# Graph attention in two layers on one core: the probabilities of head 2 turned by VectorE in six tiles of eight, and the order around head 4

## The chip, the cores and the metric

One core of a Trainium2 chip runs the whole program. The metric is device time in microseconds of one execution, from launch to end; the kernel before and the changed kernel are each run several times. Engines named below: TensorE (PE in the profile; its weight loads PEld), VectorE (DVE), ScalarE (ACT), GpSimd (POOL), and SyncE (SP), whose queue starts most of the DMAs here. Each engine takes its instructions in the order in which the program lists them, and waits where one of them has to wait.

## The reference

Sixteen graphs of 1024 nodes with 256 features pass through two layers, each with a residual. Layer 0 is masked attention with 8 heads of 32 features; layer 1 is a softmax over the products of the normed nodes, chosen by the kind of edge.

```python
h = jnp.maximum(_layernorm(x), 0.0)              # (16, 1024, 256)
Q, K, V = proj(Wq, bq), proj(Wk, bk), proj(Wv, bv)   # 8 heads of 32
scores = jnp.where(adj == 0, -inf, einsum('bhnd,bhmd->bhnm', Q, K) * 32 ** -0.5)
x = x + einsum('bno,po->bnp', heads_joined(softmax(scores) @ V), Wo) + bo

h = jnp.maximum(_layernorm(x), 0.0)
e_k = leaky_relu(einsum('bid,bjd->bij', h * a_k, h), 0.2)     # k = 0..3
scores = e_{adj - 1} where adj is 1..4, else -9e15
x = x + softmax(scores) @ h
```

In these inputs `adj` is 0 or 1, so layer 1 needs only `e_0`; a general version stands behind a test at the end of the program and isn't run.

## The kernel before, in words

Rows are worked in tiles of 128: eight tiles `t` to a batch, sixteen batches `b`, one after another in steps `s = 8 b + t`. The order of all instructions is written out by hand (`tc.manual_schedule()`, from L787 on): the loop over `s` (L839) has an inner loop over the heads `h` from 0 to 7 (L863), and each pass of it lists what is to be done at that place. Five things are under way at once: `now`, the attention tile whose scores are made; `was`, the tile before, whose products with the values are finished at heads 0 to 6; `gone`, the tile before that, whose normed result is turned; `edge` and `edge_was`, two tiles of layer 1, nine steps behind; and `piece_was` and `piece`, tiles whose queries, keys and values are projected nine steps ahead.

A head of an attention tile passes through these steps. `scores(h)` (L457) is two matmuls into one of two PSUM places, `sides[0]` or `sides[1]`; from step 9 on heads 4 and 6 use `sides[1]`, the others `sides[0]`, and the scores of layer 1 (`edge.score`, heads 0 and 2) use `sides[1]` too. `softmax_max(h)` (L469) on VectorE adds the mask, finds the maximum and writes a buffer `p`, of which there are four in turn. `softmax_exp(h - 1)` (L479) on ScalarE follows one pass later. Then the 128x1024 probabilities are turned so that keys lie on the partitions, in one of two ways:

- `turn` (L492, L585): eight TensorE transposes through PSUM, and two copies to `pT`, by ScalarE or, for a head of `MIXED`, by VectorE.
- `turn_blocks` and `place_blocks` (L379, L384): one VectorE instruction turns all blocks of 32x32 within 32 partitions, into one of three buffers `blocks`, and four DMAs of 128 KB from SP's queue bring the four groups of partitions to their places in `pT`. The keys of such a `pT` stand in another order ("blocks' order").

`combine(g)` (L522) multiplies four turned heads by their values `v` into one PSUM bank; `combine(0)` is at head 7 of the tile itself, `combine(1)` at head 4 of the next, in `block()` (L850). `combined` multiplies by the reciprocals of the sums, which GpSimd spreads (`reciprocals`), TensorE turns (`turn_reciprocals`) and ScalarE copies (`turned_reciprocals`, L518).

Values in blocks' order come from `hTm`, a copy of the turned input `hT` with its columns in that order; `values` (L335) makes 128 columns from the one and 128 from the other, and `place_of` says where a head's 32 columns lie. `MIXED` names the heads whose values are in blocks' order, (0, 1, 4, 5). `by_blocks(t)` names those that are turned by blocks: all of `MIXED`, except in tile 7 (0, 1, 4) and in tile 0 (0, 4, 5). Where a head is in the one set and not in the other, its exponential writes into a further `p` in changed order (L482).

A tile of layer 1 has its own steps: `score`, `keep` (ScalarE saves blocks of the symmetric scores in `mirror` for later tiles, L641), `softmax_max` into `sel`, `bend`, `leak`, `softmax_exp`, then in the next step `turn_blocks` and `place_blocks` at head 0, `gather(0)` (L694) in `block()`, `gather(1)` and `store` at head 7. `gather` needs the placed `pT` of all four DMAs.

Two loads on SP's queue matter. `load_queries` (L425) brings the next tile's queries `qt` (512 KB) at head 3. `load_key` (L357) brings the keys of one head (512 KB) of the next batch: `KEY_STEPS` (L78) says for each key at which half pass, counted from tile 7's head 0 as 0 and with 16 as the next batch's tile 0, it is issued.

PSUM places named `sums_place` and `brief` share one tile, `early` and `late` another (L94); the program waits by tile, so a write to one of a pair also waits for a reader of the other.

Of the kernel before, what the change touches and what calls it, by code (L numbers as in the profile page):

```python
# [17 lines left out]
P = 128  # L18
HEADS = 8
HD = 32  # L20
# [3 lines left out]
SLOPE = 0.2  # L24
NEG_INF = -9000000000000000.0
MASKED = -1e30
MIXED = (0, 1, 4, 5)
BY_BLOCKS = {7: (0, 1, 4), 0: (0, 4, 5)}


def by_blocks(t):
    return BY_BLOCKS.get(t, MIXED)


def place_of(h):

    return (h // 2 % 2) * P + (h // 4) * 2 * HD + (h % 2) * HD


FLOOR = 1e28  # L40


# [5 lines left out]
def gnn_kernel(  # L48
# [19 lines left out]
    B, N, D = x.shape  # L68
    NT = N // P
    NC = D // P  # L70
# [4 lines left out]
    LEAD = NT + 1  # L75


    KEY_STEPS = (6, 9, 10, 13, 16, 20, 22, 24)  # L78
    KEPT = LAG + 1

    const = ctx.enter_context(tc.tile_pool(name="const", bufs=1))
# [27 lines left out]
    bv_t = const.tile([P, D], F32, name="bv_t")  # L109
    bo_t = const.tile([P, D], F32, name="bo_t")  # L110

    def load_biases():
        with nc.allow_non_contiguous_dma(reason="a few hundred elements, once"):
            nc.sync.dma_start(out=bq_t, in_=bq.rearrange("(c p) -> p c", p=P))
            nc.sync.dma_start(out=bk_t, in_=bk.rearrange("(c p) -> p c", p=P))
            for k, a in enumerate((a_0, a_1, a_2, a_3)):
                nc.sync.dma_start(out=a_t[:, :, k], in_=a.rearrange("(c p) o -> p (c o)", p=P))
        for i in range(2):
            nc.sync.dma_start(
                out=bv_t[:, i * P : (i + 1) * P].rearrange("p (r d) -> p r d", r=2),  # L120
                in_=bv.rearrange("(r i d) -> i r d", i=2, r=2)[i].partition_broadcast(P),
            )
        nc.sync.dma_start(out=bo_t, in_=bo.partition_broadcast(P))

# [7 lines left out]
    def transposed_weight(name, copy=nc.vector.tensor_copy):  # L132

        rows = weight_rows[name]
        wt = const.tile([P, NC, D], F32, name=name)
        tr = ps_tr.tile([P, 4, P], F32, tag="tr", name=f"{name}_tr")
        for fc in range(NC):
            for oc in range(NC):
                nc.tensor.transpose(tr[:, fc * NC + oc, :], rows[:, oc, fc * P : (fc + 1) * P], ident)
        if name == "wvT":  # L140
            for fc in range(NC):
                nc.vector.tensor_copy(
                    wt[:, fc].rearrange("p (i r d) -> p r i d", i=2, r=2),
                    tr[:, fc * NC : (fc + 1) * NC].rearrange("p r (i d) -> p r i d", i=2),
                )
        else:
            copy(wt.rearrange("p c f -> p (c f)"), tr.rearrange("p c f -> p (c f)"))
        return wt
# [37 lines left out]
    qds, kds, vs, keysets, weights = {}, {}, {}, {}, {}  # L186

    class Piece:
# [146 lines left out]
        def values(self):  # L335
            b = self.b
            if b not in vs:
                vs[b] = graph.tile([P, NT, D], F32, tag="v", name=f"v_{b}")
            for t in range(self.n):
                ps = late if self.n == 1 else ps_tr.tile([P, D], F32, tag="tr", name="vproj")  # L340
                self.vproj = ps
                for i, hT in enumerate((self.hTm, self.hT)):
                    for fc in range(NC):
                        nc.tensor.matmul(
                            ps[:, i * P : (i + 1) * P],
                            lhsT=hT[:, fc, t * P : (t + 1) * P],
                            rhs=weights["wvT"][:, fc, i * P : (i + 1) * P],
                            start=(fc == 0),
                            stop=(fc == NC - 1),
                        )  # L350
                if self.n > 1:
                    self.biased(t)
# [423 lines left out]
    def attend_of(s):  # L776
        return Attend(*divmod(s, NT)) if 0 <= s < B * NT else None
# [9 lines left out]
    with tc.manual_schedule():  # L787
        first = [Piece(0, 0, 4), Piece(0, 4, 4)]
        piece_was, piece_next = Piece(1, 0), piece_of(0)
        now, nxt = attend_of(0), attend_of(1)  # L790
# [39 lines left out]
        piece, edge, edge_was = piece_next, None, None  # L830
# [8 lines left out]
        for s in range(B * NT + 1):  # L839
            b, t = divmod(s, NT)  # L840
# [5 lines left out]
                    load_key(b, KEY_STEPS.index(2 * (HEADS + h) + end))  # L846

            late_turn = None

            def block():  # L850
                if edge_was and not t:
                    edge_was.gather(0)
                if was:
                    was.combine(1)
                if not t and piece_was:
                    piece_was.biased()
                if was:
                    was.combined()
                if edge_was and t:
                    edge_was.gather(0)  # L860

            nxt2, edge_nxt, piece_nxt = attend_of(s + 2), edges_of(s + 1), piece_of(s + 1)
            for h in range(HEADS):  # L863
# [12 lines left out]
                    first[1].values()  # L876
                if h == 3 and edge:
                    edge.softmax_max()
                if h == 6:
                    if was:  # L880
                        was.residual()
                    norms(was, piece_nxt)
# [13 lines left out]
                if ending:  # L896
                    ending.softmax_exp(eh)

                if h == 3 and edge:
                    edge.keep(1)  # L900
                if h == 3 and was:
                    was.turned_reciprocals()
                if h == 3 and piece_was:
                    piece_was.raised(1)
                if h == 3 and edge:
                    edge.bend()


                if h == 3 and t and piece_was:
                    piece_was.biased()  # L910
                if h == 5 and was:
                    was.output()
# [8 lines left out]
                if h == 0 and t == 0 and was:  # L921
                    for half in range(2):
                        was.turn(HEADS - 3, half, nc.scalar.copy)
                    if edge:
                        edge.score(0)
                if turning and th in by_blocks(turning.t):
                    turning.turn_blocks(th)
                    turning.place_blocks(th)
                elif turning and (h, t) != (HEADS - 1, NT - 1):
                    turning.turn(th, 0)  # L930
                    turning.turn(th, 1)
# [29 lines left out]
                        was.turn_reciprocals()  # L961
                        was.add_bias()
                if h == 3:
                    if nxt:
                        nxt.load_queries()
                    if edge:
                        edge.leak()
                    if piece_was:
                        piece_was.halve(1)
                    if edge_was:  # L970
                        edge_was.load_nodes()
                    if nxt:
                        nxt.flag()
                        nxt.mask()
                if h == 4:
                    block()
                if h == 5:
                    if piece_was:
                        piece_was.write_queries()
                    if edge_nxt:  # L980
                        edge_nxt.prepare()
                    if nxt2:
                        nxt2.load()
# [18 lines left out]
            gone, was, now, nxt = was, now, nxt, nxt2  # L1002
            edge_was, edge = edge, edge_nxt
            piece_was, piece = piece, piece_nxt
# [7 lines left out]
        for i in range(1, len(tiles) + 2):  # L1012
            edge = tiles[i] if i < len(tiles) else None
# [75 lines left out]
```

## Time and profile before

| what | us |
|---|---|
| median of three runs | 3014.63 (3009.04 to 3017.09) |
| the profiled execution | 3012.56 |
| its span, first to last instruction | 3010.7 |
| granted TensorE clock | 0.998 of full speed |

| instruction (line) | engine | count | mean ns |
|---|---|---|---|
| maximum of a head, `softmax_max` (L473) | VectorE | 1024 | 1209 |
| exponential of a head (L490) | ScalarE | 1024 | 1196 |
| block transpose of a head, `blocks<-p` (L381) | VectorE | 488 | 1240 |
| block transpose of `sel` (L381) | VectorE | 120 | 1241 |
| transposes on TensorE, `trp<-ident,p` (L590) | TensorE | 4352 | 274 |
| their copies (L591) | ScalarE | 1024 | 592 |
| their copies (L591) | VectorE | 64 | 685 |
| `pT<-blocks`, 128 KB, issue to landing | SP's queue | 2432 | 3600 (median) |
| `qt<-qd`, 512 KB, issue to landing | SP's queue | 128 | 4700 (median) |
| `k<-kd`, 512 KB, issue to landing | SP's queue | 128 | 6800 (median) |

How to read it: a line of a timeline gives the start in us from the span's start, the length, the engine, the line of the program, the operation, what is written and what is read with shapes, the count of instructions merged, and in brackets how long the engine had been idle before and what ended that. Matmuls overlap, so the distance from one start to the next tells more than a length (274 ns is one transpose's, but eight take about 0.8 us). The views of waits count idle time by what ended it. A page's share of busy time is a mean over stages with different limits; the timelines show which wait ends last in each.

### The profile page before, as it was taken

Reading aid. Unit: us, or ns where it says so; the run is one execution under the profiler, and the core shown is the slowest. Engines: PE = TensorE matmul, PEld = TensorE weight load, DVE = VectorE, ACT = ScalarE, POOL = GpSimd, SP = SyncE. Lnnn points to the kernel's source line nnn. Section 1 sums busy time; section 2 is a strip of 40 time slices with the busy share of each in tenths; the row PEclk is TensorE's granted clock in tenths of the full one; section 3 lists DMA queues with packets and bytes.
Section 4 is the critical chain, followed back from the end, with each engine's and each line's share of the span. In section 5 each row is a group of like instructions: output and inputs, shape, how many; then the busy total and the mean of one; then the engine's idle time right before and its main releaser. Section 6 shows DMA issues by size and latency. Waiting matters only on the chain. (4 is left out here: it accounts for less than half of the span.)

```text
span 3010.7 us, 95592 instructions
## 1 busy us (share of the span) xinstructions
PE 2888.7 (96%) x36466; PEld 2218.8 (74%) x36466; DVE 2517.8 (84%) x4421; ACT 2602.5 (86%) x5159; POOL 2167.4 (72%) x2999
## 2 busy tenths in 40 slices
PE   7889999999999999999999999999999999999998
PEld 5767777777777777777777777777777777777664
DVE  5878888788888888888888788888888888888885
ACT  5989989899898889889899898998989888898882
POOL 4667877777787787778778777777877777786542
PEclk9999999999999999999999999999999999999999
DMA  7787878878778887887877788787787878878763
GB/s 257 235 258 215 244 240 241 256 226 266 230 228 255 238 268 216 243 253 227 274 227 232 243 240 262 223 261 241 226 259 240 266 216 241 258 224 263 198 175 102
DMA packets 616255, 712.41 MB, mean 237 GB/s; under 512 B 65328, under 2 KB 546992, under 8 KB 615792
## 3 DMA queue, kind: packets, MB, share of 16 engines
q1 hardware_dynamic: 546720, 494.08, 55.5%
q0 software_dynamic: 66960, 210.04, 21.6%
q8 instruction: 293, 4.80, 0.7%
q10 hardware_dynamic: 2112, 2.10, 0.2%
q14 instruction: 170, 1.39, 0.1%
HBM read 252.98 MB, written 134.22 MB: 129 GB/s over the span
## 5 line engine op out<-in xcount | busy, mean ns | idle before, releaser
L473 DVE CUSTOM_DVE_ANT_0 p<-s,neg 128x1024 f32<-128x1024 f32 x1024 | 1237.9, 1209 | 320.2 <-PE s L461 291.9
L490 ACT ACTIVATE p<-p,nmx 128x1024 f32<-128x1024 f32 x1024 | 1218.3, 1196 | 53.3 <-DVE nmx L473 51.1
L461 PE MATMUL s<-k,qt 128*128 128x512 f32 x2048 | 743.7, 445 | 56.0 <-DMA k<-kd 28.4
L591 ACT COPY pT<-trp 128x512 f32<-128x512 f32 x1024 | 549.9, 592 | 99.9 <-PE trp L590 99.6
L381 DVE STREAM_TRANSPOSE blocks<-p 128x1024 f32<-128x1024 f32 x488 | 605.0, 1240 | 12.3 <-ACT p L680 10.6
L590 PE MATMUL trp<-ident,p 128*128 128x128 f32 x4352 | 571.5, 274 | 20.4 <-ACT p L490 13.0
L590 PEld LDWEIGHTS trp<-ident,p 128*128 128x128 f32 x4352 | 502.6, 141 | 105.0 <-ACT p L490 26.5
L526 PE MATMUL acc<-pT,v 128*32 128x128 f32 x16384 | 509.7, 274 | 11.3 <-ACT full L309 8.8
L526 PEld LDWEIGHTS acc<-pT,v 128*32 128x32 f32 x16384 | 454.7, 110 | 83.4 <-issue 36.9
L698 PE MATMUL acc<-h,pT 128*32 128x256 f32 x8192 | 508.4, 381 | 2.1 <-DMA pT<-blocks 2.0
L441 POOL TENSOR_SCALAR neg<-adj 128x1024 bf16<-128x1024 int32 x128 | 467.7, 3654 | 11.9 <-ACT neg L453 1.8
L461 PEld LDWEIGHTS s<-k,qt 128*128 128x128 f32 x2048 | 312.0, 190 | 182.7 <-issue 91.1
L676 POOL TENSOR_TENSOR sel<-sel,less 128x1024 f32<-128x1024 f32 x120 | 287.6, 2396 | 194.6 <-ACT less L665 194.6
L698 PEld LDWEIGHTS acc<-h,pT 128*32 128x32 f32 x8192 | 263.3, 110 | 191.9 <-issue 50.3
L633 PE MATMUL s<-h1T,ha 128*128 128x512 f32 (+2 forms) x744 | 272.8, 490 | 2.6 <-ACT h1T L569 0.8
L490 ACT ACTIVATION_READ_ACCUMULATOR p<-p,nmx 128x1 f32 x1024 | 211.8, 207 | 0.0
L330 POOL DMA_DIRECT2D kd<-halves x240 | 171.7, 764 | 35.4 <-POOL halves L314 35.4
L314 POOL TENSOR_TENSOR halves<-full,halves 128x256 fp32r<-128x256 f32 x240 | 176.3, 735 | 20.0
L647 ACT COPY mirror<-s 128x128 f32<-128x128 f32 (+3 forms) x208 | 75.9, 392 | 125.5 <-DVE top L656 104.4
L324 POOL DMA_DIRECT2D qd<-halves x240 | 177.3, 785 | 7.1
L674 POOL TENSOR_SCALAR less<-top 128x1 f32<-128x1 f32 x120 | 31.8, 265 | 204.3 <-DVE top L656 204.1
L633 PEld LDWEIGHTS s<-h1T,ha 128*128 128x128 f32 x744 | 126.7, 190 | 70.5 <-issue 45.2
(117 smaller groups left out, 4314.5 us busy)
## 6 DMA issues: line engine op xcount, KB each, us to landing
pT<-blocks SPq DMA_DIRECT2D x2432, 128.0 KB, 3.6
qt<-qd SPq DMA_DIRECT2D x128, 512.0 KB, 4.7
k<-kd SPq DMA_DIRECT2D x128, 512.0 KB, 6.8
adj<-in_adj POOLq DMA_DIRECT2D x127, 512.0 KB, 6.2
qd<-halves POOLq DMA_DIRECT2D x240, 256.0 KB, 3.8
kd<-halves POOLq DMA_DIRECT2D x240, 128.0 KB, 4.2
xb<-in_x POOLq DMA_DIRECT2D x128, 128.0 KB, 4.9
x1d<-x SPq DMA_DIRECT2D x128, 128.0 KB, 5.1
```

Source lines behind the costliest of these rows:

```text
L324: nc.gpsimd.dma_start(out=qds[self.b][self.first, oc].rearrange("p u w n -> p u (w n)"), in_=halves.unsqueeze(1).to_broadcast([P, 2, 2 * P]),)
L381: nc.vector.transpose(blocks.rearrange("p b j q -> p j b q"), p)
L441: nc.gpsimd.tensor_scalar(self.neg, self.adj, 0.0, MASKED, ALU.is_equal, ALU.mult)
L461: nc.tensor.matmul(self.ps[:, cols], lhsT=self.qt[:, h, :], rhs=keysets[self.b][h][:, cols], start=True, stop=True,)
L473: nc.vector.tensor_tensor_reduce(out=p, in0=sides[h in self.second], in1=self.neg, scale=-SCALE, scalar=FLOOR, op0=ALU.add, op1=ALU.min, a ...
L490: nc.scalar.activation(to, of, AF.Exp, bias=nmx, scale=-1.0, accum_out=self.sums[:, h : h + 1])
L526: nc.tensor.matmul(sums_place[r * HD : (r + 1) * HD, g * P : (g + 1) * P], lhsT=vs[self.b][:, j, place_of(h) : place_of(h) + HD], rhs=self ...
L590: nc.tensor.transpose(tr[:, j, :], p[:, jj * P : (jj + 1) * P], ident)
L591: copy(pT[:, half * 4 : half * 4 + 4, :], tr)
L633: nc.tensor.matmul(self.side[:, cols], lhsT=self.ha[:, c, :], rhs=h1T[:, c, cols], start=(c == 0), stop=(c == NC - 1),)
L676: nc.gpsimd.tensor_tensor(self.sel, self.sel, self.less, ALU.subtract)
L698: nc.tensor.matmul(self.sums[a * HD : (a + 1) * HD, :], lhsT=self.pT[:, j, a], rhs=h1s[self.b][:, j, :], start=(j == 0), stop=(j == NT - 1),)
```

## The change

- Head 2 joins `MIXED`: its values are made from `hTm` (160 columns from it, 96 from `hT`), its columns move, and the weights and bias are laid out by runs of heads (`RUNS`) with four copies and four DMAs where there were two.
- In tiles 1 to 6 (`five`) head 2 is turned by blocks. In tiles 0 and 7 it isn't, so that its exponential writes into a further `p` in changed order; in tile 7 the copies of its turn are VectorE's (in tile 0 they were already).
- In tiles 1 to 6 `block()` comes ahead of head 2's turn and head 4's scores and not behind them; `biased` (VectorE) comes ahead of head 3's maximum; `keep(1)` (ScalarE) comes behind the reciprocals' copy and `raised(1)`.
- `load_queries` moves from head 3 to head 5, except in tile 7.
- The fourth key's load moves from step 13 to step 12, the start of tile 7's head 6 and not its end.

```diff
@@ -24,7 +24,8 @@
 SLOPE = 0.2
 NEG_INF = -9000000000000000.0
 MASKED = -1e30
-MIXED = (0, 1, 4, 5)
+MIXED = (0, 1, 2, 4, 5)
+PLACES = MIXED + (3, 6, 7)
 BY_BLOCKS = {7: (0, 1, 4), 0: (0, 4, 5)}
 
 
@@ -33,10 +34,10 @@
 
 
 def place_of(h):
-
-    return (h // 2 % 2) * P + (h // 4) * 2 * HD + (h % 2) * HD
-
-
+    return PLACES.index(h) * HD
+
+
+RUNS = ((0, 0, 3), (3, 4, 2), (5, 3, 1), (6, 6, 2))
 FLOOR = 1e28
 
 
@@ -75,7 +76,7 @@
     LEAD = NT + 1
 
 
-    KEY_STEPS = (6, 9, 10, 13, 16, 20, 22, 24)
+    KEY_STEPS = (6, 9, 10, 12, 16, 20, 22, 24)
     KEPT = LAG + 1
 
     const = ctx.enter_context(tc.tile_pool(name="const", bufs=1))
@@ -115,10 +116,10 @@
             nc.sync.dma_start(out=bk_t, in_=bk.rearrange("(c p) -> p c", p=P))
             for k, a in enumerate((a_0, a_1, a_2, a_3)):
                 nc.sync.dma_start(out=a_t[:, :, k], in_=a.rearrange("(c p) o -> p (c o)", p=P))
-        for i in range(2):
+        for to, first, n in RUNS:
             nc.sync.dma_start(
-                out=bv_t[:, i * P : (i + 1) * P].rearrange("p (r d) -> p r d", r=2),
-                in_=bv.rearrange("(r i d) -> i r d", i=2, r=2)[i].partition_broadcast(P),
+                out=bv_t[:, to * HD : (to + n) * HD],
+                in_=bv[first * HD : (first + n) * HD].partition_broadcast(P),
             )
         nc.sync.dma_start(out=bo_t, in_=bo.partition_broadcast(P))
 
@@ -138,10 +139,10 @@
             for oc in range(NC):
                 nc.tensor.transpose(tr[:, fc * NC + oc, :], rows[:, oc, fc * P : (fc + 1) * P], ident)
         if name == "wvT":
-            for fc in range(NC):
+            rows = tr.rearrange("p (f o) n -> p f (o n)", f=NC)
+            for to, first, n in RUNS:
                 nc.vector.tensor_copy(
-                    wt[:, fc].rearrange("p (i r d) -> p r i d", i=2, r=2),
-                    tr[:, fc * NC : (fc + 1) * NC].rearrange("p r (i d) -> p r i d", i=2),
+                    wt[:, :, to * HD : (to + n) * HD], rows[:, :, first * HD : (first + n) * HD]
                 )
         else:
             copy(wt.rearrange("p c f -> p (c f)"), tr.rearrange("p c f -> p (c f)"))
@@ -339,12 +340,13 @@
             for t in range(self.n):
                 ps = late if self.n == 1 else ps_tr.tile([P, D], F32, tag="tr", name="vproj")
                 self.vproj = ps
-                for i, hT in enumerate((self.hTm, self.hT)):
+                edge = len(MIXED) * HD
+                for cols, hT in ((slice(0, edge), self.hTm), (slice(edge, D), self.hT)):
                     for fc in range(NC):
                         nc.tensor.matmul(
-                            ps[:, i * P : (i + 1) * P],
+                            ps[:, cols],
                             lhsT=hT[:, fc, t * P : (t + 1) * P],
-                            rhs=weights["wvT"][:, fc, i * P : (i + 1) * P],
+                            rhs=weights["wvT"][:, fc, cols],
                             start=(fc == 0),
                             stop=(fc == NC - 1),
                         )
@@ -846,6 +848,7 @@
                     load_key(b, KEY_STEPS.index(2 * (HEADS + h) + end))
 
             late_turn = None
+            five = now and 2 in by_blocks(t)
 
             def block():
                 if edge_was and not t:
@@ -876,6 +879,8 @@
                     first[1].values()
                 if h == 3 and edge:
                     edge.softmax_max()
+                if h == 3 and five and piece_was:
+                    piece_was.biased()
                 if h == 6:
                     if was:
                         was.residual()
@@ -896,17 +901,19 @@
                 if ending:
                     ending.softmax_exp(eh)
 
-                if h == 3 and edge:
+                if h == 3 and edge and not five:
                     edge.keep(1)
                 if h == 3 and was:
                     was.turned_reciprocals()
                 if h == 3 and piece_was:
                     piece_was.raised(1)
+                if h == 3 and edge and five:
+                    edge.keep(1)
                 if h == 3 and edge:
                     edge.bend()
 
 
-                if h == 3 and t and piece_was:
+                if h == 3 and t and not five and piece_was:
                     piece_was.biased()
                 if h == 5 and was:
                     was.output()
@@ -923,6 +930,8 @@
                         was.turn(HEADS - 3, half, nc.scalar.copy)
                     if edge:
                         edge.score(0)
+                if five and h == 4:
+                    block()
                 if turning and th in by_blocks(turning.t):
                     turning.turn_blocks(th)
                     turning.place_blocks(th)
@@ -961,7 +970,7 @@
                         was.turn_reciprocals()
                         was.add_bias()
                 if h == 3:
-                    if nxt:
+                    if nxt and t and not five:
                         nxt.load_queries()
                     if edge:
                         edge.leak()
@@ -972,9 +981,11 @@
                     if nxt:
                         nxt.flag()
                         nxt.mask()
-                if h == 4:
+                if h == 4 and not five:
                     block()
                 if h == 5:
+                    if nxt and (five or not t):
+                        nxt.load_queries()
                     if piece_was:
                         piece_was.write_queries()
                     if edge_nxt:
```

## The prediction

> **What bounds the kernel now.** I read the summary first, for how full each engine is:
>
> ```profile
> PE 2888.7 (96%) x36466; PEld 2218.8 (74%) x36466; DVE 2517.8 (84%) x4421; ACT 2602.5 (86%) x5159; POOL 2167.4 (72%) x2999
> ```
>
> TensorE (PE) is busy almost throughout, which says where to look and not what a saved microsecond is worth. The chain of waits holds only the last 20 us, so I read the timelines of one tile instead: batch 8, tile 4, from head 0's scores at 1568.62 to the next tile's at 1590.74. TensorE around head 4, where the change works:
>
> ```profile
> 1576.60 0.72 PE L461 MATMUL s<-k,qt 128*128 128x512 f32 x2
> 1577.16 1.04 PE L590 MATMUL trp<-ident,p 128*128 128x128 f32 x8
> 1578.24 0.73 PE L461 MATMUL s<-k,qt 128*128 128x512 f32 x2
> 1578.91 1.95 PE L526 MATMUL acc<-pT,v 128*32 128x128 f32 x64
> 1580.68 1.91 PE L698 MATMUL acc<-h,pT 128*32 128x256 f32 x32
> 1582.52 0.73 PE L461 MATMUL s<-k,qt 128*128 128x512 f32 x2
> ```
>
> That is: head 3's scores, head 2's eight transposes, head 4's scores, `combine(1)`, `gather(0)`, head 5's scores. The transposes cost 0.79 us from start to start where nothing waits (tile 1: 1510.46 to 1511.25); here 1.08, because head 4's scores wait for ScalarE's mirror copy, which itself waited on VectorE:
>
> ```profile
> 1577.61 0.59 ACT L647 COPY mirror<-s 128x512 f32<-128x512 f32 x1 [0.98 <-DVE top L656]
> ```
>
> VectorE (DVE) has its largest gap there too, waiting for head 5's scores:
>
> ```profile
> 1583.29 1.23 DVE L473 CUSTOM_DVE_ANT_0 p<-s,neg 128x1024 f32<-128x1024 f32 x1 [1.23 <-PE s L461]
> ```
>
> Next the view that decides: what `gather(0)` stands on. It multiplies the graph tile's probabilities (`sel`), which VectorE turns at the tile's start and SP's DMAs put in place. SP's queue from head 4's pieces on, and the gather of tile 5:
>
> ```profile
> 1588.58 3.98 SPq L386 DMA_DIRECT2D pT<-blocks  x4
> 1592.61 0.61 SPq L552 DMA_DIRECT2D x1d<-x  x1
> 1593.33 2.58 SPq L386 DMA_DIRECT2D pT<-blocks  x4
> 1596.49 0.60 SPq L708 DMA_DIRECT2D out<-h  x1
> ```
>
> ```profile
> 1602.73 2.78 PE L698 MATMUL acc<-h,pT 128*32 128x256 f32 x32
> ```
>
> The four issues for `sel` follow at 1597.21, 4.4 us after VectorE began that transpose (1592.76). They need 2.6 us and land some 2.7 later: 1602.5. The gather took 2.78 us where it takes 1.91: it started and then stood for a piece. So TensorE is full, but in this order the gather comes just as its pieces arrive. Over batches 2 to 14 the trace gives the last `sel` piece 11.3 us after head 0's scores in tiles 2 to 6 and the gather's start at 12.6, 12.3, 12.1, 11.9, 11.8. The tiles last 22.96, 22.65, 22.32, 22.16, 22.05, 21.92 (1 to 6), 22.21 (7) and 26.58 us (0).
>
> **The change, part by part.** The sum goes against the profiled run's own 3012.56 us (span 3010.7); the median of the three runs is 2.07 above it.
>
> *Tiles 1 to 6, engine work.* TensorE loses eight transposes and, as head 4's scores now come after the gather, the mirror wait: about 0.8 us in tile 1 and 1.0 to 1.2 in the others. ScalarE loses two copies (592 ns each). VectorE gains a block transpose, 1.16 us from start to start (1589.55 to 1590.72). From head 2's maximum at 1574.06 to the next tile's at 1596.11 are 22.05 us, of which 0.31, 1.23, 0.20 and 0.67 are idle: 19.64 of work. With 1.16 more it is 20.8, and with the last wait, which needs a score product behind each maximum, 21.5. If engines alone decided, tile 1 would save 0.8 and the other five 3.85 together: 4.65 us a batch.
>
> For the price of the turn, the Trainium skill (VectorE: DVE Perf Modes, The three transpose paths) gives 311 ns for a 128x128 bf16 tile on VectorE against 390 on TensorE. An estimate from that page is 8 x 0.311 = 2.49 us for a head, against the change; the rows have 1.24 for all eight, and the measurement decides. By the page VectorE would carry 96 x 1.25 = 120 us more, and 0.9 us of gap a tile would hide 86 of it, leaving the sum 34 higher.
>
> *Tiles 1 to 6, order.* `block()` moves ahead of head 4's scores, so the gather could start 1.4 to 1.6 us sooner: in tile 4 after 1576.60 + 0.56 + 1.77, some 10.4 us into the tile. Its last piece comes at 11.3. So the gather waits, and behind it on TensorE stand head 4's scores, and behind those VectorE's maxima of heads 4 to 7. VectorE has less done by then than now: today head 4's maximum (1580.52) is over before the gather ends; afterwards it comes behind it. Walked as a loop: from the gather's end to head 4's maximum 0.75 us, then maxima 4 and 5 (2.3), residual and statistics (1.6, 1584.61 to 1586.16), maximum 6 (1.1), head 4's block transpose (1.24): 7.0. From that transpose's end to the last `sel` piece the trace has 13.5 us in every tile from 1 to 6 (13.45 to 13.62); then the gather, 1.75. Together 22.25 us, against a mean of 22.22 in tiles 2 to 6. Carried from tile 1, whose gather has 1.5 us to spare, the batch ends 0.2 us ahead. The unknown is the 13.5. From below, fourteen issues of 0.65, a gap of 0.6 and a landing of 2.7 make 12.4, where engines decide again; from above, every fourth issue as slow as the 3.98 group shows, 14.0. I take 13.6, nearest the rows, as the queue's fourteen issues stay and the DMAs get 384 transfers more (512 packets a tile): +0.3 a batch, 15 batches, **+4.5**. Batch 0 has no gather, and saves some 0.5 in six tiles: **-3**.
>
> *Their cover.* Head 2's four issues need 2.6 us of SP behind head 1's; SP is idle there today after `qt` (1583.45). `qt` now follows them, at about 1586, and with a landing of 4.7 comes at 1590.7, where head 0's scores want it: no margin, nothing in the sum, and 0.5 a tile (45 us) if it is late. Head 2's pieces land about 1588, when `combine(0)` starts (1588.88 today). The earlier bias on VectorE (0.35) fills a wait of 0.31; reciprocals and `raised(1)` (0.76) fill ScalarE's 0.98. Value products have 160 and 96 columns for 128 and 128: nothing. Two DMAs and two 0.42 us copies in the preparation: +0.5.
>
> *Tile 7.* Head 2 now belongs to the heads in blocks' order but isn't turned by blocks here: its exponential writes in another order, as head 5's does:
>
> ```profile
> 1652.65 2.27 ACT L490 ACTIVATE p<-p,nmx 128x1024 f32<-128x1024 f32 x1
> ```
>
> 2.27 instead of 1.15, and into a fifth `p` where there are four. That place was head 0's, which VectorE reads until 1643.12:
>
> ```profile
> 1641.88 1.24 DVE L381 STREAM_TRANSPOSE blocks<-p 128x1024 f32<-128x1024 f32 x1
> ```
>
> So it starts at 1643.2 and not 1642.05, and ends at 1645.4. The transposes wait till then, and head 4's scores come at 1646.25, not 1644.59: 1.66 us, and 16 tiles make **+26.6**. Without the wait for the place it is 0.56 a tile, 9; with the maximum at 2.1, 34. The two copies that VectorE takes over (685 ns each) lie in its 1.23 gap; without it they would cost 1.37 a tile.
>
> *Tile 0.* Head 3's key is issued a step sooner, ahead of head 4's pieces and `keep`:
>
> ```profile
> 1668.80 0.92 PE L461 MATMUL s<-k,qt 128*128 128x512 f32 x2 [3.44 <-DMA k<-kd]
> ...
> 1671.08 1.20 PE L461 MATMUL s<-k,qt 128*128 128x512 f32 x2
> ```
>
> This is the longest such wait; over the batches head 3's scores start at 9.22 us, and at 7.61 without it. Its issue moves from about +2 us to -4.5, and lands in time. But `gather(0)` in this tile stands on pieces landing at 12.86, and those come sooner only by the issue taken from ahead of them (0.65 to 1.56) and lighter traffic. I take 1.2 us of 15 tiles: **-18**, between 0 and -36 (1.6 and 0.8 of head 4's key). Head 2's longer exponential (1.06) ends at about 1668.1; the recT and bias copies behind it end at 1668.9, before the gather (1672.21). With that cover gone: +16.
>
> Sum: 3012.6 + 4.5 - 3 + 0.5 + 26.6 - 18 = 3023.2; on the scale of the median **3025**.
>
> **Rivals.** *The engines decide* (faster): the `sel` pieces come with the chain at 12.4 or less, and tiles 1 to 6 save 4.65 a batch, 74 us in all. For it: TensorE's 96% and the gaps named. Against: the gather of 2.78. 3012.6 - 74 + 26.6 - 18 + 0.5 + 2.1 = 2950. It decides below about 12.7 us.
> *Traffic stretches the chain* to 14.0, or `qt` is late: 0.4 more in five tiles of 15 batches, +30: 3055. For it: DMA busy 77 to 81% in these tiles before 1.8 us more of each DMA engine's time (512 packets of 56 ns over 16); against: that falls in a lighter stretch.
> *Tile 7 doesn't wait for the place*: 9 for 26.6: 3007.
>
> **How the numbers follow.** Chances: forecast 0.43 (3008 to 3042), engines 0.30, traffic 0.15, no wait in tile 7 0.12. About 0.3% (9 us) is what this measurement can tell from no change: below 3005.6 faster, above 3023.7 slower. Faster: 0.29 + 0.06 + 0.01 = 0.36. Same: 0.14 + 0.06 = 0.20. Slower: 0.28 + 0.15 + 0.01 = 0.44. From 2945 to 3052 about 0.13 is left out below and 0.07 above.
>
> **What would show it.** After: the gather of tiles 2 to 6 still starting or stretching until about 11.3 us, with VectorE waiting for head 4's scores; tile 7 longer by 1.7 us with transposes waiting for an exponential of 2.2; the key wait of tile 0 gone. Wrong if the gather runs in 1.91 us at 10.4 and tiles take 21.5, or if head 0's scores wait for `qt`.

## The result, and the profile after

The changed kernel takes 3105.84 us in the median (3102.46 to 3112.24, 4 runs), the kernel before 3011.84 on the same chip (3005.76 to 3017.09): 1.0309 times as long, 95% interval 1.0287 to 1.0331. It is slower, as forecast, by far more than the range allowed. The profiled execution took 3102.46 us with a span of 3100.7, so 90.0 us more between first and last instruction than in the profile of before.

Where they lie follows from the starts of head 0's scores, tile by tile (means over batches 2 to 14, us):

| stage | before | after | difference | in all |
|---|---|---|---|---|
| batch 0, whole | 158.0 | 202.6 | +44.6 | +44.6 |
| tile 0 | 26.58 | 25.29 | -1.29 | x13: -16.8 |
| tiles 1 to 6 together | 134.06 | 136.34 | +2.28 | x13: +29.6 |
| tile 7 | 22.21 | 23.88 | +1.67 | x13: +21.7 |
| batch 1; batch 15 and the ends | | | | +3.0; +7.9 |

Tile 0 of batch 0 alone lasts 21.6 to 28.0 us over all profiled kernels, so a few us of batch 0's 44.6 need not be the change's; its tiles 1 to 6 went from 112.3 to 155.1.

The summary of the page has moved as the work has: TensorE has fewer instructions and a smaller share, VectorE carries the block transposes:

```profile
PE 2881.1 (93%) x35698; PEld 2204.4 (71%) x35698; DVE 2622.6 (85%) x4551; ACT 2549.6 (82%) x4935; POOL 2166.7 (70%) x2999
```

TensorE in batch 8, tile 4, whose head 0 starts at 1628.06; the timeline shows head 3's scores, `combine(1)`, `gather(0)`, and heads 4 and 5 in one line:

```profile
1636.06 0.71 PE L463 MATMUL s<-k,qt 128*128 128x512 f32 x2
1636.77 2.05 PE L528 MATMUL acc<-pT,v 128*32 128x128 f32 x61
1638.55 0.38 PE L700 MATMUL acc<-h,pT 128*32 128x256 f32 x1
...
1638.72 2.07 PE L700 MATMUL acc<-h,pT 128*32 128x256 f32 x31
1640.72 1.19 PE L463 MATMUL s<-k,qt 128*128 128x512 f32 x4
```

The gather starts 10.5 us into this tile, and head 4's scores, which came at 9.6 us before, stand behind it at 12.7. VectorE's gap of 1.23 us ahead of head 5's maximum is gone, and one of 0.53 stands ahead of head 4's.

At the end of the tile `combine(0)` and the next tile's first scores followed each other without a stand before:

```profile
1588.88 1.93 PE L526 MATMUL acc<-pT,v 128*32 128x128 f32 x64
1590.74 0.73 PE L461 MATMUL s<-k,qt 128*128 128x512 f32 x2
```

After, the loads come late there. SP's queue, then TensorE's `combine(0)`, the next scores, and one tile later `combine(1)`:

```profile
1645.44 0.54 SPq L430 DMA_DIRECT2D qt<-qd  x1
1647.84 2.99 SPq L388 DMA_DIRECT2D pT<-blocks  x4
1650.88 0.60 SPq L554 DMA_DIRECT2D x1d<-x  x1
1651.59 4.60 SPq L388 DMA_DIRECT2D pT<-blocks  x4
1656.29 0.62 SPq L710 DMA_DIRECT2D out<-h  x1
```

```profile
1647.66 2.02 PE L528 MATMUL acc<-pT,v 128*32 128x128 f32 x64
1649.97 0.70 PE L463 MATMUL s<-k,qt 128*128 128x512 f32 x2 [0.29 <-DMA qt<-qd]
...
1661.29 2.73 PE L528 MATMUL acc<-pT,v 128*32 128x128 f32 x59 [2.23 <-DMA pT<-blocks]
```

The queries, issued at 1645.44, hold the next tile's first scores by 0.29 us; the four pieces of head 5, of which the issue alone takes 4.60 us, hold that tile's `combine(1)` by 2.23, and it lasts 25.4 us. The view of waits sums such stands up (us in total, times, longest):

```profile
PE acc L528 <- DMA pT<-blocks: 63.7, 41, 5.4
...
PEld acc L700 <- DMA pT<-blocks: 25.1, 69, 2.6
...
PEld acc L528 <- DMA pT<-blocks: 18.1, 9, 5.0
...
DVE blocks L383 <- DMA pT<-blocks: 14.3, 22, 1.8
...
PE s L463 <- DMA qt<-qd: 9.6, 15, 1.4
...
PE s L463 <- DMA k<-kd: 6.4, 7, 1.5
```

Before, the largest such rows were the keys' and the gather's; no other row for pieces had more than 2.2 us, and the queries had 1.1:

```profile
PE s L461 <- DMA k<-kd: 28.4, 23, 3.4
...
PEld acc L698 <- DMA pT<-blocks: 10.9, 35, 0.8
```

The stands of more than 4 us at products with the values are batch 0's, one in each of its tiles 1 to 6. One of these tiles, with VectorE's turn of head 2 first, then GpSimd's two query writes and its load of graph rows, SP's load of queries, and `combine(0)`:

```profile
153.75 1.24 DVE L383 STREAM_TRANSPOSE blocks<-p 128x1024 f32<-128x1024 f32 x1
...
156.65 1.47 POOL L325 DMA_DIRECT2D qd<-halves  x2
...
157.85 0.83 POOL L434 DMA_DIRECT2D adj<-in_adj  x1
...
159.10 1.47 SPq L430 DMA_DIRECT2D qt<-qd  x1
...
160.11 0.59 PE L528 MATMUL acc<-pT,v 128*32 128x128 f32 x4 [0.85 <-ACT full L310]
...
165.34 3.00 PE L528 MATMUL acc<-pT,v 128*32 128x128 f32 x52 [4.64 <-DMA pT<-blocks]
```

`combine(0)` makes four matmuls and stands for 4.64 us until head 2's pieces are there. They were issued from 156.18 to 159.05 and landed at 158.7, 160.6, 162.9 and 165.2. The same product in batch 0 before, whose wait is for another engine:

```profile
117.30 2.16 PE L526 MATMUL acc<-pT,v 128*32 128x128 f32 x64 [0.94 <-ACT full L309]
```

Tile 7's reordered exponential and the scores of heads 2, 3 and 4 in the next tile 0:

```profile
1705.76 2.13 ACT L492 ACTIVATE p<-p,nmx 128x1024 f32<-128x1024 f32 x1 [1.87 <-DVE blocks L383]
```

```profile
1726.78 0.71 PE L463 MATMUL s<-k,qt 128*128 128x512 f32 x2
...
1729.20 0.71 PE L463 MATMUL s<-k,qt 128*128 128x512 f32 x2
...
1731.10 0.73 PE L463 MATMUL s<-k,qt 128*128 128x512 f32 x2
```

The exponential waits for VectorE's read of its place and takes 2.13 us; head 3's scores no longer wait for their key (7.67 us into tile 0 in the mean, 9.22 before).

### The profile page after: what moved, and what is told of

Read it like the earlier page. It is cut to its first block, busy times and chain, and to the rows that moved or that the text cites. A ratio compares the mean times of both kernels' runs of the same rounds, so it can differ in the third digit from the quotient of the medians.

```text
span 3100.7 us, 95063 instructions
## 1 busy us (share of the span) xinstructions
PE 2881.1 (93%) x35698; PEld 2204.4 (71%) x35698; DVE 2622.6 (85%) x4551; ACT 2549.6 (82%) x4935; POOL 2166.7 (70%) x2999
## 3 DMA queue, kind: packets, MB, share of 16 engines
q0 software_dynamic: 66960, 210.04, 21.2%
## 5 line engine op out<-in xcount | busy, mean ns | idle before, releaser
L475 DVE CUSTOM_DVE_ANT_0 p<-s,neg 128x1024 f32<-128x1024 f32 x1024 | 1232.9, 1211 | 299.8 <-PE s L463 180.8
L492 ACT ACTIVATE p<-p,nmx 128x1024 f32<-128x1024 f32 x1024 | 1247.6, 1222 | 95.9 <-DVE nmx L475 60.6
L383 DVE STREAM_TRANSPOSE blocks<-p 128x1024 f32<-128x1024 f32 x584 | 723.3, 1238 | 26.5 <-DMA pT<-blocks 14.3
L528 PE MATMUL acc<-pT,v 128*32 128x128 f32 x16384 | 560.5, 278 | 86.3 <-DMA pT<-blocks 63.7
L528 PEld LDWEIGHTS acc<-pT,v 128*32 128x32 f32 x16384 | 485.3, 112 | 185.2 <-issue 67.2
L593 ACT COPY pT<-trp 128x512 f32<-128x512 f32 x800 | 427.6, 585 | 175.0 <-PE trp L592 174.7
L700 PE MATMUL acc<-h,pT 128*32 128x256 f32 x8192 | 542.4, 382 | 14.8 <-ACT full L310 9.3
L592 PE MATMUL trp<-ident,p 128*128 128x128 f32 x3584 | 474.1, 275 | 47.4 <-ACT p L492 40.3
L592 PEld LDWEIGHTS trp<-ident,p 128*128 128x128 f32 x3584 | 414.5, 141 | 120.5 <-ACT p L492 54.4
L700 PEld LDWEIGHTS acc<-h,pT 128*32 128x32 f32 x8192 | 302.9, 110 | 199.9 <-issue 48.1
L512 POOL COPY wide<-rec 128x256 f32<-128x256 f32 x128 | 68.1, 532 | 163.8 <-DVE rec L510 163.4
```

Source lines behind the costliest of these rows:

```text
L383: nc.vector.transpose(blocks.rearrange("p b j q -> p j b q"), p)
L475: nc.vector.tensor_tensor_reduce(out=p, in0=sides[h in self.second], in1=self.neg, scale=-SCALE, scalar=FLOOR, op0=ALU.add, op1=ALU.min, a ...
L492: nc.scalar.activation(to, of, AF.Exp, bias=nmx, scale=-1.0, accum_out=self.sums[:, h : h + 1])
L528: nc.tensor.matmul(sums_place[r * HD : (r + 1) * HD, g * P : (g + 1) * P], lhsT=vs[self.b][:, j, place_of(h) : place_of(h) + HD], rhs=self ...
L592: nc.tensor.transpose(tr[:, j, :], p[:, jj * P : (jj + 1) * P], ident)
L593: copy(pT[:, half * 4 : half * 4 + 4, :], tr)
```

## The experiments

The theory after the result: the gather, tile 7 and tile 0 did what was forecast, and the loss beyond it comes from head 2's own pieces and the queries behind them, landing late at `combine(0)` and the next scores, worst in batch 0. Its rivals: the new order alone costs it; the added DMA traffic costs it. All times are medians, ratios are against the kernel before on the same chip (3015.2 to 3015.8 us there). The changed kernel's 3105.84 comes from a chip on which the kernel before took 3011.84, so a difference to it is uncertain by some 4 us.

**Batch 0's head 2 turned by TensorE again** (in the changed kernel).

```diff
-def by_blocks(t):
-    return BY_BLOCKS.get(t, MIXED)
+def by_blocks(t, b=1):
+    return BY_BLOCKS.get(t, MIXED if b else (0, 1, 4, 5))
```

> The changed kernel, but in batch 0 head 2 is turned by TensorE (the order around head 4 and all else stay). Theory 'late pieces' (head 2's four DMAs come so late in the tile that combine(0) at head 7 stands for them; in batch 0 they meet the queries' writes and the next adjacency load): the stands of about 5 us in combine(0) of batch 0 go, its tiles 1 to 6 fall from 25.2-26.4 us to about 19.5-20.5, and the run is 35 to 45 us shorter than the changed kernel (about 3063). Theory 'order' (block() ahead of head 4's scores is what is slow where the scores alternate between the two PSUM places): batch 0 stays at 25 us a tile and the run within 8 us of 3106.

Measured: 3086.68 us, ratio 1.0228 (1.0202 to 1.0254): 19 us below the changed kernel, where 35 to 45 were expected. Tiles 1 to 6 of batch 0 last 22.1 us, with 25.9 in the changed kernel and 18.7 before. The stands at `combine(0)` are gone, but half of the loss is not. ScalarE and TensorE show what stays there, in two lines of their timelines:

```profile
140.87 2.13 ACT L492 ACTIVATE p<-p,nmx 128x1024 f32<-128x1024 f32 x1 [0.81 <-DVE blocks L383]
```

```profile
143.27 3.47 PE L528 MATMUL acc<-pT,v 128*32 128x128 f32 x64 [3.21 <-ACT recT L522]
```

A head of `MIXED` that isn't turned by blocks has the exponential of 2.13 us, with its wait for a place, and `combine(1)` waits for the reciprocals' copy behind it: the experiment brought tile 7's cost into batch 0. A later run takes that out.

**Head 2's exponential in plain order in tile 7** (that head's elements stand in another order there).

```diff
-            if (h in MIXED) != (h in by_blocks(self.t)):
+            if (h in MIXED) != (h in by_blocks(self.t)) and (h, self.t) != (2, NT - 1):
```

> The changed kernel, but in tile 7 head 2's exponential is written in place and in the old order (the change of order of head 2's probabilities in tile 7 is left out, so what is computed there differs). Theory of the prediction (the longer exponential and its wait for a fifth place p cost 1.66 us in each of 16 tiles 7): tile 7 falls from 23.9 to about 22.2 us and the run by 22 to 30 us (about 3080). Rival (tile 7 is longer because its pieces or loads come late after the crowded tile 6): under 8 us.

Measured: 3088.49 us, 1.0247 (1.0225 to 1.0269): 17 us lower, short of the 22 to 30 expected. Tile 7 falls from 23.88 to 22.30 us (22.21 before), so the reordered exponential is nearly its whole loss; tile 0 rises from 25.29 to 26.24, so 0.95 us of the 1.58 is given back there.

**`combine(0)` moved to the next tile's head 0**, to give the pieces more time.

```diff
+                    if was:
+                        was.combine(0)
                 if h == 1:
...
-                    if now:
-                        now.combine(0)
```

> The changed kernel, but combine(0) comes in the next tile's head 0, behind its scores, the turn of head 6 and the first half of the layer 1 scores, about 3 us later. Theory 'late pieces': combine(0) no longer stands: some 1.4 us a batch in tiles 2 to 6 (about 20 us) and most of the 5 us in each of batch 0's tiles (25 to 35 us) go; 3050 to 3065. Theory 'DMAs are full' (the traffic itself sets the pace, and a wait that is removed comes back at the next transfer): less than 15 us. Theory 'order': no change, as the gather's wait stays.

Measured: 3302.09 us, 1.0954 (1.0916 to 1.0992). A miss against every expectation, and it doesn't speak on the pieces: with the products between heads 0 and 1, VectorE's maxima wait 431.8 us in all for scores (180.8 in the changed kernel), and the scores wait 187.9 us for the queries (9.6), above all in batch 0 (26 to 28 us a tile). Why the queries come so much later there was not taken apart.

**The key's earlier step alone, in the kernel before.**

```diff
-    KEY_STEPS = (6, 9, 10, 13, 16, 20, 22, 24)
+    KEY_STEPS = (6, 9, 10, 12, 16, 20, 22, 24)
```

> The kernel before with the fourth key's load at step 12, nothing else. Theory: tile 0's wait for that key goes and the layer 1 pieces come some 1.2 us sooner in 14 or 15 batches: 12 to 25 us faster than before (about 2994). Rival (the load only moves its traffic in front of head 4's pieces, and tile 0 is set by these): within 6 us.

Measured: 3003.63 us (8 runs), 0.9964 (0.9948 to 0.998). Tile 0 falls from 26.58 to 25.80 us; 15 of them make 11.7, and the median is 11.6 lower, at the edge of the 12 to 25 expected. Of the parts that ran alone it is the one that pays, and this version is the fastest of all that ran.

**Queries back at head 3**, ahead of head 2's pieces (in the changed kernel).

```diff
-                    if nxt and t and not five:
+                    if nxt:
                         nxt.load_queries()
...
-                    if nxt and (five or not t):
-                        nxt.load_queries()
```

> The changed kernel with load_queries back at head 3 in all tiles, ahead of head 2's pieces on SP's queue. Theory 'late pieces' (what is issued last in the middle of the tile lands too late for whoever needs it at the tile's end): the wait of the next tile's head 0 for its queries (0.2 us a tile, some 16 us) goes, but head 2's pieces come 0.55 us of issue and 1.8 us of DMA time later and combine(0) stands 0.5 to 1 us more in tiles 2 to 6: 20 to 60 us slower than the changed kernel (3125 to 3165). Rival 'the queries' wait is what costs' (the move of the load is the mistake): 15 to 45 us faster than the changed kernel.

Measured: 3182.38 us, 1.055 (1.0533 to 1.0568), more than any theory gave. In tiles 2 to 6 the next scores follow `combine(0)` in 0.2 us, so the wait for the queries is gone; but `combine(0)` itself lasts 2.9 to 3.8 us from first to last matmul, where it needs 1.7. Head 2's last piece lands 1.3 us behind its start in the median tile, and on its start (0.1 ahead) in the changed kernel. The view of waits:

```profile
PE acc L528 <- DMA pT<-blocks: 144.5, 96, 5.7
...
PEld acc L528 <- DMA pT<-blocks: 67.9, 43, 6.0
```

What the queries gain, head 2's pieces lose, and more: both can't be in time in this place of the queue.

**The order of before with head 2 by blocks** (changed kernel; `block()`, `biased` and `keep(1)` back in their places).

```diff
-                if five and h == 4:
-                    block()
...
-                if h == 4 and not five:
+                if h == 4:
                     block()
```

> The changed kernel with the order of before around heads 3 and 4 (block() behind head 4's scores in all tiles, biased and keep(1) where they were); head 2 still turned by blocks, loads still moved. Theory 'late pieces': TensorE loses the transposes but then waits for the mirror copy, the gather finds its pieces there, and the tile's end still stands for head 2's pieces and the queries: tiles 2 to 6 at 22.2 to 22.9 us, batch 0 at 22 to 25 us a tile, 3060 to 3100. Theory 'order' (the gather and head 4's scores put late are the loss): 3030 or less, tiles 2 to 6 under 22.

Measured: 3124.4 us, 1.0355 (1.0325 to 1.0385): 18.6 more than the changed kernel and above what either theory gave. Batch 0's tiles 1 to 6 last 24.7 to 25.9 us with stands of 3.5 to 5.0 at `combine(0)` all the same. So the late pieces don't come from the new order; with head 2 by blocks it is the better of the two.

**The new order with head 2 turned by TensorE** (kernel before, in tiles 1 to 6).

```diff
+            five = now and 1 <= t <= 6
...
+                if five and h == 4:
+                    block()
...
-                if h == 4:
+                if h == 4 and not five:
                     block()
```

> The kernel before with the new order alone (block() ahead of head 2's turn and head 4's scores in tiles 1 to 6, the bias ahead of head 3's maximum, keep(1) behind the reciprocals); head 2 on TensorE and all loads as before. Loop of the prediction: the gather stands till about 11.3 us, then the transposes (0.8) and head 4's scores come behind it: 22.25 + 0.8 = 23 us in tiles 2 to 6, 3 to 5 us more a batch, and 3 us a tile in batch 0: 3075 to 3110, with no wait for queries and none in combine(0). If order costs nothing by itself, within 10 us of before.

Measured: 3071.26 us, 1.0185 (1.0167 to 1.0204), 4 us below the range expected. `combine(0)` takes 1.66 us and the next scores follow in 0.2; batch 0's tiles 1 to 5 last 18.75 us in the mean (18.68 before; its tile 6 takes 21.0 for 18.9), where the expectation had 3 us more. So the order isn't free by itself: 56 us, nearly all in batches with a gather. The gather starts 10.4 to 11.1 us into tiles 2 to 6 and waits for its last piece; head 4's scores, behind it and behind head 2's transposes, come at 14.0 us instead of 9.7. The view of waits, where before has 10.9 us and 35 times:

```profile
PEld acc L698 <- DMA pT<-blocks: 27.3, 77, 1.6
```

**The traffic alone**: four more DMAs of 128 KB behind head 4 in tiles 1 to 6 of the kernel before, into DRAM that nothing reads.

```diff
+                if h == 4 and now and 1 <= t <= 6:
+                    for a in range(NB):
+                        nc.sync.dma_start(out=spare[:, a * NT * HD : (a + 1) * NT * HD], in_=now.blocks[a * HD : (a + 1) * HD])
```

> The kernel before with four more DMAs of 128 KB in head 4 of tiles 1 to 6 (head 1's blocks written once more, to a spare place in DRAM that nobody reads), so that the traffic and the issues of the change are there without anyone waiting for them. Theory 'late pieces': under 10 us slower than before, in batch 0 too. Theory 'traffic' (DMAs are full, and 384 transfers more make every landing later, the layer 1 pieces above all): 20 to 50 us slower.

Measured: 3018.88 us (10 runs), 1.0018 (1.0005 to 1.0032): 3.6 us for 2.6 us of issues and 512 KB in each of 96 tiles. The traffic rival falls, as far as writes to DRAM stand for head 2's, which go to `pT`; what costs is that something waits for the pieces.

**Batch 0 with head 2 by TensorE and in plain order** (head 2's elements stand in another order there).

```diff
-            if (h in MIXED) != (h in by_blocks(self.t, self.b)):
+            if (h in MIXED) != (h in by_blocks(self.t, self.b)) and (h, self.b) != (2, 0):
```

> The changed kernel with batch 0's head 2 turned by TensorE and its exponential written in plain order there (so batch 0's head 2 is not turned rightly: its elements stand in another order). Theory: the 3.3 us by which batch 0's tiles stayed longer in the first run of this part (22.1 us against 18.75 with the new order alone) is the exponential of head 2 in blocks' order, 2.13 us where a plain one takes 1.15, waiting 0.8 us for its place and holding the reciprocals' copy and so combine(1): as in tile 7. Then batch 0's tiles 1 to 6 fall to 18.7 to 19.2 us, and the kernel to 3061 to 3070, 38 to 45 below the changed one. Rival: the new order or the later queries cost it; then the tiles stay at 21.5 to 22.1 and the time at 3080 to 3088.

Measured: batch 0's tiles 1 to 6 last 19.0 us, inside the theory's numbers, and the batch 164.1 instead of 202.6. `combine(0)` there, in one line of the timeline:

```profile
145.41 2.16 PE L528 MATMUL acc<-pT,v 128*32 128x128 f32 x64 [0.84 <-ACT full L310]
```

So 38.5 of batch 0's 44.6 us are head 2's turn by blocks. The time of the kernel didn't follow: 3090.33 us (3078.08 to 3093.9), 1.025, outside what either theory gave. The profiled execution is the shortest of the four, 24.4 us of span below the changed kernel's, and its batches 1 to 14 last 186.2 us in the mean against 185.1: part of the gain is given back in later batches. It is given back at the same place: in tile 1 of batches 2 to 14 every head's scores start within 0.03 us of the changed kernel's, but head 2's last piece lands at 21.2 us into the tile and not at 20.4, though it is issued no later, and `combine(0)` lasts 2.31 us and not 1.66. Why the pieces land later there isn't shown.

**GpSimd's load of graph rows behind `combine(0)` in batch 0** (changed kernel).

```diff
-                    if nxt2:
+                    if nxt2 and b:
                         nxt2.load()
...
                         now.combine(0)
+                    if nxt2 and not b:
+                        nxt2.load()
```

> The changed kernel with GpSimd's load of the graph rows (adj, 512 KB) behind combine(0) in batch 0, from head 5's place. Theory: in batch 0 that load and the query writes are issued within 1 us of head 2's four pieces and hold them in the DMA engines (landing 2.5 to 6 us after their issue); with it out of the way combine(0) stands 2 us and not 4.7, batch 0's tiles last 22.5 to 24 us and not 25.9, 12 to 20 us in all: 3086 to 3094. Rival: the pieces are late because head 2's turn itself comes late, behind the block and head 4's scores; then batch 0's tiles stay within 0.7 us of what they were and the time at 3100 to 3110.

Measured: 3097.42 us, 1.0264 (1.0233 to 1.0295), between the two expectations. Batch 0 lasts 191.5 us, 11.1 less; its tiles 1 to 6 last 21.2 to 24.6 us (139.9 together, 155.1 in the changed kernel), and in one of them `combine(0)` stands for 2.26 us, where it stood for some 4.7 in all, and the next scores for 1.19 for the queries. The load is a part of what holds the pieces; the larger part stays, and was not taken apart further (the query writes, at 156.65 in the changed kernel's tile above, are the next to suspect).

**Tiles 1 to 6 of batches 1 to 15, and tile 0's key**: batch 0 in plain order as above, with tile 7's exponential plain as well.

```diff
+            ... and (h, self.b) != (2, 0) and (h, self.t) != (2, NT - 1):
```

> The run on batch 0 in plain order, with head 2 plain in tile 7 of every batch too (its elements stand in another order there): what is left of the change is tiles 1 to 6 of batches 1 to 15 and tile 0's key. Theory: the losses add, so the time is that of the run on batch 0 less the 17 us that tile 7 alone gave: 3044 to 3053. That is +2.3 us a batch in tiles 1 to 6 (35 us) with tile 0's gain all but given back. Rival: the losses overlap and the rest costs little: below 3035; or tile 7's loss is given back whole at the next key: above 3058.

Measured: 3057.69 us, 1.0145 (1.0123 to 1.0166), 5 us above the theory's numbers and just short of the rival's 3058. With batch 0 and tile 7 taken out, 42 us are left, though the key's step has won some 12 by itself: tiles 1 to 6 last 137.5 us a batch, 3.4 more than before, so their loss stands by itself.

## Why the prediction was wrong

Its sum, term by term, against the two profiles (the means of batches 2 to 14, taken for 15 batches):

| term | forecast | measured |
|---|---|---|
| tiles 1 to 6, batches 1 to 15 | +4.5 | 2.28 x 15 = +34 |
| batch 0 | -3 | +44.6 |
| tile 7 | +26.6 | 1.67 x 15 = +25 |
| tile 0 | -18 | -1.29 x 15 = -19 |
| preparation, rest | +0.5 | about +5 |

**The step that failed is "Their cover"**: head 2's pieces, said to land "about 1588, when `combine(0)` starts", and the queries, with "no margin, nothing in the sum", were both priced at nothing. The text's own sign of being wrong, head 0's scores waiting for `qt`, is there. Tiles 2 to 6 of a batch, summed (means of batches 2 to 14, us), show it in the kernels that differ in one thing:

| kernel | head 0's scores to `combine(0)` | its first to its last matmul | from there to the next scores |
|---|---|---|---|
| before | 101.80 | 8.29 | 1.01 |
| before, with the traffic alone | 101.90 | 8.29 | 1.01 |
| before, with the new order alone | 104.92 | 8.29 | 1.01 |
| changed, with the order of before | 103.52 | 9.05 | 2.01 |
| changed | 101.86 | 9.70 | 2.06 |
| changed, with queries at head 3 | 98.76 | 16.84 | 1.06 |

`combine(0)` is stretched only where head 2 goes by blocks, and the next scores come later only where the queries are issued at head 5. In the changed kernel that is 1.41 for the pieces and 1.05 for the queries (of which the trace puts a part down to VectorE), 2.5 us a batch and all of what tiles 2 to 6 lost. By the prediction's figures the last piece lands 19.4 us into the tile, 0.9 ahead of `combine(0)`; measured it lands at 20.3 in the mean, 0.1 ahead, and between 0.8 ahead and 0.9 behind in eight tiles of ten. So `combine(0)` takes more than 1.9 us in 23 of 65 tiles, where it never did before, and landing on time in the mean is landing late in many tiles.

**Batch 0** failed by the same step: the term was built on what TensorE saves, with no arrival checked. Only batches with a gather were looked at, where GpSimd issues its query writes some 20.0 us into the tile and the load of graph rows at 21.8, behind head 2's pieces (issued from 15.1 on). In batch 0 two writes of 256 KB go out at 13.3 to 14.6 us and the load of 512 KB at 14.3 to 15.3, among these pieces, and the last of them lands 5.9 to 7.2 us behind its issue (3.2 in the later batches). The stand recurs in its tiles 1 to 6, and is gone with head 2 on TensorE; how much of it each of GpSimd's transfers makes is shown for the load alone (11 us of the batch, 15 of its tiles 1 to 6).

**Tiles 1 to 6, order** held. The gather started 10.6 to 11.4 us into tiles 2 to 6 in the means (10.4 forecast), its last matmul came at 12.9 to 13.5 us (11.3 and 1.75 make 13.05), and up to `combine(0)` the tiles came out even, as the loop of 22.25 us had it. The rows cited for it, 13.5 us of chain, carried (13.4 to 14.0 after). That they come out even is a balance: the new order alone costs 3.1 us a batch up to `combine(0)`, and head 2's turn, taken from TensorE, gives them back.

**Tile 7** held in place, mechanism and size (1.67 us for 1.66), shown by the run with its exponential plain. That it would give 17 us and not 25 if removed, since tile 0 takes part of it back, was not in the text.

**Tile 0** held in size: -1.29 for -1.2. In the kernel before, the same step is worth 0.78 a tile, so some of the 1.29 comes from elsewhere in the change, which wasn't taken apart.

**The rivals.** *The engines decide* fell: the pieces set the gather's end. *Traffic stretches the chain, or `qt` is late* fell in its first half (3.6 us for the traffic alone), and was right in its second, though the queries are about 1 us of each batch's 2.5. It had 30 us, and left out head 2's own pieces and batch 0. *Tile 7 doesn't wait* fell to the 1.87 us of wait.

## What to carry to other kernels

A path through DMAs in place of an engine's copy needs its arrival checked against the first reader, with the spread of the landing and not its median, and in each stage that is run: here the stage without the second layer's work gave half of the loss. Four extra transfers a tile cost 3.6 us when nobody waited for them. Where something did, they and the queries pushed behind them cost some 75 by the profiles (38.5 in batch 0 and 2.5 in each later batch), so it is the margin at the reader that is to be priced, not the traffic. Such a sum isn't what removing a stand gives back: without batch 0's 38.5 the median fell by 15.5 only. When two loads share a queue with no margin, moving one ahead only chooses which is late. What would help, an earlier producer or a later reader off the serial part, isn't shown here: the one run that moved the reader took 3302.09 us.

## What the runs showed of the hardware

Stands of TensorE cost more than their length. In batch 0 of the changed kernel, the 60 matmuls behind a stand took twice their time:

```profile
113.45 3.63 PE L528 MATMUL acc<-pT,v 128*32 128x128 f32 x60 [4.54 <-DMA pT<-blocks]
117.01 1.22 PE L463 MATMUL s<-k,qt 128*128 128x512 f32 x2
...
119.42 0.71 PE L463 MATMUL s<-k,qt 128*128 128x512 f32 x2
```

Sixty-four take 1.95 us where nothing is waited for, and two of the scores 0.71 to 0.73, as they do again 6 us later. The windows of each kernel (length, busy time with instructions of PE, PEld, DVE, ACT and POOL, granted clock, share of the DMA engines, GB/s) show the clock, first before and then after:

```profile
110.00:160.00 50.00, 44.69 (x603) 37.19 (x598) 45.74 (x81) 46.96 (x97) 36.78 (x50) 1.00 0.79 244
```

```profile
110.00:160.00 50.00, 35.90 (x400) 29.93 (x400) 33.31 (x60) 32.12 (x67) 24.43 (x32) 0.86 0.62 185
```

So `combine(0)` in batch 0 takes 8.4 us from first to last matmul where it took 1.9: 4.7 of stand, and most of the rest the lower clock, which is 0.50 from 113.45 to 117.10 us and 1.00 from 119.40 to 121.00. The Trainium skill (TensorE: Matmul & The Clock Gate, Part 1) says that the clock falls to half after an idle stretch of about 3.4 us; the stands above 4 us with half speed behind them agree. Shorter stands do it too here, though not always. With the graph rows' load moved, batch 0 has

```profile
134.34 3.59 PE L528 MATMUL acc<-pT,v 128*32 128x128 f32 x60 [2.26 <-DMA pT<-blocks]
```

at a clock of 0.52, and one tile earlier the same 60 matmuls take 1.94 us behind a stand of 1.49, at 1.00. In the changed kernel the stand of 2.23 us at 1661.29, shown above, has a clock of 0.50 behind it from 1662.07 to 1665.48, while over 400 to 1600 us, with several stands of 1.9 to 2.2 us, it is 1.00. So no length of stand below 3.4 us is shown to be safe, and a wait of 2 us or more may have to be priced with slow matmuls behind it.

The same four issues of 128 KB on SP's queue (head 5's) took 2.56 us in one tile and 4.60 in the next. Over batches 2 to 14 of the changed kernel the median is 2.66, and 10 of 572 took more than 4; which resource held them, the traces don't show.
